# A two-way cross-attention kernel: setup opens with Wk's transposes and batch 0's keys, and batch 0's values are made by block products

## The chip, the cores and the metric

The kernel runs on one NeuronCore of one Trainium2 chip, in float32. The metric is the device time of one execution in microseconds. Five engines work in parallel from instruction streams of their own and meet through semaphores: PE (TensorE, matmuls, with PEld for its weight loads), DVE (VectorE), ACT (ScalarE), POOL (GpSimd) and SP (SyncE, which here only issues DMA transfers; ACT and POOL issue some too).

## The reference

There are 16 batches. `x` is 16 x 100 x 640; the context is 16 x 722 x 384, of which 718 rows are encoder rows and the last four are token rows. There are 8 heads of 80.

```python
enc, ca = ctx[:, :718, :], ctx[:, 718:, :]
query, keyt, valt = x @ Wq, enc @ Wk, enc @ Wv
hs = mha(query, keyt, valt)                       # 100 queries, 718 keys
ca_q1 = einsum('btc,th->bch', ca, Wq_ca)[:, indices, :]
ca_hs1 = mha(ca_q1, x, x)                         # second branch, first attention
ca_hs2 = mha(ca_hs1 @ Wq, ca @ Wk_ca, ca @ Wv_ca) # second attention, four keys
out = (hs + ca_hs2) @ Wout + b_out + x
```

The second branch is folded with weights: products of Wk_ca, Wq and the tokens (`k2`, `m`) are made once for all batches.

## The kernel before, in words

Each batch's encoder rows, transposed, are held as three thirds of 240 rows by three blocks of 128 channels (`a_raw(enc, u, c)`). Keys are computed as kT (channels on partitions, in five chunks of 128: four of packed heads and a last one for what is left of the heads), values as vs (rows on partitions, in two halves of 120 of each third).

**Two ways to the same products.** The direct way runs one matmul for each of the nine pairs of a third and a channel block, as in `first_keys` (L627, matmuls recorded at L609) and `first_values` (L414, L421). The other way is by blocks: `Values` (L456) and `Keys` (L499) walk a plan of 15 products in place of 18. Operands of these are sums of blocks: of the encoder input, by `enc_sums` (L527, recorded at L548, on POOL, thirteen for a batch), and of the weights, by `weight_sums` (L552, recorded at L572, on DVE, twelve each for Wv and Wk). A product is two matmuls; what it gives is copied by ACT or added by DVE into kT or vs. `go(n)` issues the next n products of the plan.

**Setup.** It runs from the top of the function to the batch loop at L1386:

- Loads. SP issues most, in the order of the text (`in_order`), ACT issues the six of Wv. Eight completion semaphores are used in turn by all loads from SP and ACT.
- Five matmuls on zeros (L1258), then `first_values` for four of batch 0's six blocks of rows (24 matmuls), and beside them Wv's block sums on DVE. Three of Wv's sums have no room of their own yet and go to `wv_there` (L397), which batch 1's value products read; ACT copies them home in batch 1 (L1531).
- `k2` (30 matmuls), masked by DVE (L1279); five `m_ps` tiles of five matmuls (L1293), each copied by DVE (L1301) and stored by SP; `keys(m)` (L765), in which POOL masks the five m tiles (L770).
- `Second` is the second branch of a batch: `products` makes y_ps (five matmuls, L798) and DVE reduces it to g; `scores1` (L826) is seven operations of POOL on 100 x 800 (L833, L840); `softmax1` is a maximum on DVE by two transposes and reductions (L722 to L752) and a subtraction (L850); `exponentials1` is on ACT (L853); `softmax2` makes z_ps on PE (L860) and divides it on DVE (L871).
- Fifteen transposes turn Wk back from its packed transposed form (w_ps, L1316); DVE copies Wq into its packed order (L1327, L1335, fifteen copies); then `first_keys` (45 matmuls, the last nine of them `last_keys`), va_ps (L1360) and the 25 matmuls of `queries` (L585).

Up to L1385 a scheduler of the framework decides the order on each engine; from there on (`manual_schedule`) the order of the text is the order on every engine.

**The batch loop.** For each batch: three groups of `scores` (L659), between them DVE's running maxima (`larger`, L1416 and L1428), then `softmax2`, the next batch's `products`, and a stretch in which value products of this batch and key products of the next alternate on PE while the first softmax runs on DVE and ACT (`Maximum`, `subtract`, `exponential`), then `last_keys`, r_ps (row sums, L1586) and a_ps (L1604). Batch 0 has a branch of its own: it makes the remaining 12 value matmuls directly (L421 again), and only batch 1's keys by blocks.

**Accumulators.** PSUM tiles come from three rings of two: `pair` (two banks each), `psumk` and `psum1` (one bank each); `psum` takes from them in turn in setup. A tile of a ring is free when the last reader of the tile two before it has finished: `z_ps`, `y_ps` and the two halves of v_psD all come from `psum1`.

## Time and profile before

| | |
|---|---|
| time, median of three runs | 928.01 us (927.03 to 928.19) |
| profiled execution | 927.66 us, span 925.9 us |
| PE busy | 917.3 us of the span (99%) |
| DVE, ACT, POOL busy | 650.4, 375.4, 620.9 us |
| 0 to 28.42 us (to the end of m_ps) | PE busy 26.32 us, DMA 257 GB/s |
| 28.42 to 60.86 (to batch 0's scores) | PE busy 32.01 us, DMA 140 GB/s |
| 60.86 to 100.71 (batch 0) | PE busy 39.15 us, DVE 30.64, POOL 33.64 |
| 100.71 to 156.80 (batch 1) | PE busy 56.09 us of 56.09 |

The chain of waits lists, backwards from the last instruction, what each step waited for; its rows are start, length, engine, tile and line. The timeline lists the instructions of each engine with start, busy time, line, operation, tiles, shape and number, and behind them in brackets the idle time ahead and what ended it. Times are from the start of the span. PE's matmuls leave two records each.

### The profile page before, as it was taken

What the parts mean: (1) busy time and instruction counts of PE and PEld (TensorE: products, weight loads), DVE (VectorE), ACT (ScalarE), POOL (GpSimd) and SP (SyncE); (2) the same over time, 40 slices, a digit from 0 to 9 for tenths busy, and PEclk for the clock granted to TensorE, in tenths of its full rate; (3) what the DMA queues carried; (4) which work ended last, traced back from release to release, by engine and by line L of the source; (5) the groups of instructions that cost most, each with busy time, mean ns of one, the idle gap of its engine ahead of it and who ended that gap; (6) DMA issues with size and microseconds to landing.
All of it is one profiled execution on the core that took longest, in us unless ns stands there. A gap on an engine that the chain in (4) does not pass through costs nothing.

```text
span 925.9 us, 26078 instructions
## 1 busy us (share of the span) xinstructions
PE 917.3 (99%) x11163; PEld 778.3 (84%) x11163; DVE 650.4 (70%) x1116; ACT 375.4 (41%) x649; POOL 620.9 (67%) x646
## 2 busy tenths in 40 slices
PE   9999999999999999999999999999999999999998
PEld 6997879788887979888798887988888888888865
DVE  2358896878729786685966759578792887828783
ACT  2244534434424453532434334344541445425451
POOL 5748788566945878477684856745796566955624
PEclk9999999999999999999999999999999999999999
DMA  8613352051401504140131402204140151401331
GB/s 265 201 47 87 73 120 73 6 142 34 109 12 37 138 6 110 43 123 20 49 94 43 132 12 74 72 12 133 43 109 10 34 139 36 109 12 44 86 84 32
DMA packets 68956, 69.50 MB, mean 75 GB/s; under 512 B 26088, under 2 KB 62632, under 8 KB 68840
## 3 DMA queue, kind: packets, MB, share of 16 engines
q1 hardware_dynamic: 67512, 66.51, 26.9%
q8 instruction: 88, 1.44, 0.6%
q10 hardware_dynamic: 864, 0.98, 0.3%
q0 software_dynamic: 464, 0.34, 0.2%
q14 instruction: 28, 0.23, 0.1%
HBM read 62.14 MB, written 8.94 MB: 77 GB/s over the span
## 4 chain that ended last, share of the span: by engine, by line
PE 96%; DVE 2%; DMA 1%; ACT 0%; issue 0%; POOL 0%; ACTq 0%; DVEq 0%
PE s_ps L659 12%; PE v_psA L480 10%; PE v_psB L480 8%; PE kT_ps L609 8%; PE k_psA L511 8%; PE a_ps L1604 7%; PE q_ps L585 7%; PE k_psB L511 6%; PE r_ps L1586 4%; PE v_psC L480 3%; PE k_psC L511 3%; PE v_ps L421 2%; PE y_ps L798 2%; PE o_psy L1127 2%; PE v_psD L480 2%; PE v_psE L480 2%
## 5 line engine op out<-in xcount | busy, mean ns | idle before, releaser
L833 POOL TENSOR_TENSOR e<-ca,g 100x800 f32<-100x800 f32 x64 | 99.2, 1560 | 95.6 <-DVE most L1416 90.7
L548 POOL TENSOR_TENSOR enc<-enc 128x240 f32<-128x240 f32 x135 | 104.3, 782 | 19.4 <-ACT qp L593 10.1
L480 PE MATMUL v_psA<-wv_sb,enc 128*120 128x320 f32 x352 | 109.6, 434 | 0.1
L840 POOL TENSOR_TENSOR e<-e,e 100x800 f32<-100x800 f32 x48 | 97.7, 2035 | 3.8
L659 PE MATMUL s_ps<-qp,kT 32*120 32x100 f32 x3072 | 97.5, 263 | 0.0
L659 PEld LDWEIGHTS s_ps<-qp,kT 32*120 32x120 f32 x3072 | 94.7, 179 | 2.1 <-issue 0.2
L480 PE MATMUL v_psB<-wv_sb,enc 128*120 128x320 f32 x296 | 91.7, 432 | 0.0
L1404 DVE TENSOR_TENSOR st<-st,over 120x1600 f32<-120x1600 f32 x47 | 89.9, 1913 | 0.0
L511 PE MATMUL k_psA<-enc,wk_sb 128*128 128x240 f32 x360 | 87.8, 367 | 0.6 <-DVE kT L451 0.5
L511 PEld LDWEIGHTS k_psA<-enc,wk_sb 128*128 128x128 f32 x360 | 68.2, 190 | 17.7 <-DVE kT L451 0.9
L480 PEld LDWEIGHTS v_psA<-wv_sb,enc 128*120 128x120 f32 x352 | 63.3, 183 | 23.0 <-DVE vs L451 1.0
L1416 DVE TENSOR_TENSOR most<-most,st 120x800 f32<-120x800 f32 x64 | 64.8, 1013 | 23.3 <-ACT st L681 22.2
L1412 ACT ACTIVATE st<-st 120x1600 f32<-120x1600 f32 x48 | 74.0, 1541 | 8.4 <-DVE st L1404 8.0
L1428 DVE TENSOR_TENSOR most<-st 120x800 f32<-120x800 f32 x16 | 16.9, 1059 | 81.1 <-ACT st L687 81.1
L511 PE MATMUL k_psB<-enc,wk_sb 128*128 128x240 f32 x300 | 73.1, 366 | 0.1
L480 PEld LDWEIGHTS v_psB<-wv_sb,enc 128*120 128x120 f32 x296 | 54.2, 183 | 21.7
L1604 PE MATMUL a_ps<-st,vs 120*64 120x100 f32 (+1 forms) x1536 | 69.5, 250 | 0.0
L585 PE MATMUL q_ps<-xT,wq_sb 128*128 128x200 f32 x400 | 69.1, 333 | 0.0
L1604 PEld LDWEIGHTS a_ps<-st,vs 120*64 120x64 f32 (+1 forms) x1536 | 66.4, 137 | 2.7 <-issue 2.7
L585 PEld LDWEIGHTS q_ps<-xT,wq_sb 128*128 128x128 f32 x400 | 67.9, 190 | 0.2
L940 POOL TENSOR_TENSOR hs<-hs,pb 128x500 f32<-128x500 f32 x48 | 65.5, 1364 | 3.8
L687 ACT COPY st<-s_ps 120x800 f32<-120x800 f32 x64 | 49.7, 829 | 44.0 <-PE s_ps L659 44.0
(195 smaller groups left out, 1861.3 us busy)
## 6 DMA issues: line engine op xcount, KB each, us to landing
pb<-p_d SPq DMA_DIRECT2D x32, 400.0 KB
enc<-in_enct SPq DMA_DIRECT2D x30, 240.0 KB
enc<-in_enct SPq DMA_DIRECT2D x15, 360.0 KB
xT<-in_xt SPq DMA_DIRECT2D x8, 500.0 KB
rest<-in_enct SPq DMA_DIRECT2D x31, 120.0 KB
xn<-in_x SPq DMA_DIRECT2D x11, 320.0 KB
wide_d<-p_d SPq DMA_DIRECT2D x16, 200.0 KB
pb<-wide_d SPq DMA_DIRECT2D x16, 200.0 KB
```

Of the source, the lines that this page charges most:

```text
L480: nc.tensor.matmul(at[0][j][:KN, : H // 2], a_form(self.enc, f)[:, j * KN : (j + 1) * KN], wv_there.get(f, wv_sb[:, W_AT[f]]), start=first ...
L511: nc.tensor.matmul(at[:, i * KT : (i + 1) * KT], wk_sb[:, W_AT[f], i], a_form(self.enc, f), start=(first and i == 0), stop=last, skip_grou ...
L548: first = nc.gpsimd.tensor_tensor(out, left, right, op)
L585: nc.tensor.matmul(q_ps[:, : 2 * S].rearrange("p (j s) -> p j s", j=2), wq_sb[:, c, n * P : (n + 1) * P], xT[:, :, c, :], start=(c == 0), ...
L609: nc.tensor.matmul(bank[:, i * KT : (i + 1) * KT], weights[c], a_raw(enc, u, c), start=(i == 0 and c == 0), stop=(c == CC - 1), skip_group ...
L659: nc.tensor.matmul(s_ps[bank][:n, 256 * a + lo : 256 * a + lo + rhs.shape[-1]], kT[rows, c, u, j * KN : (j + 1) * KN], rhs, start=bank not ...
L833: first = nc.gpsimd.tensor_tensor(to, self.ca[:, t, :].unsqueeze(1).to_broadcast([S, NH, S]), g[:, :, t].unsqueeze(2).to_broadcast([S, NH, ...
L840: nc.gpsimd.tensor_tensor(e, e, to, ALU.add)
L940: nc.gpsimd.tensor_tensor(self.hs2, self.hs2, to, ALU.add)
L1404: return engine.tensor_tensor(st[i], st[i], top.over[:KN].unsqueeze(1).to_broadcast([KN, 2, ROWS]), ALU.subtract,)
L1412: nc.scalar.activation(st[i], st[i], AF.Exp, scale=SCALE)
L1604: nc.tensor.matmul(wides[64 * e : 64 * e + 64, h // 2], slot(i, h, FIRST[e], 64), st[i // 2][: KEYS[i], i % 2, h * S : (h + 1) * S], start ...
```

## The change

- The hand-written order holds from the beginning of the function; `in_order` and the `issue_after` groups go.
- Loads: Wk (transposed, packed by head) comes first, its four even heads on ACT's queue, and on SP's, behind the three thirds of channel block 0 of batch 0's encoder input, the four odd heads and the rest; then the other thirds, the tokens, Wk_ca, Wq transposed, Wv in one transfer, x, Wq and ca_0. Wv_ca goes into the room of Wq transposed once m_ps is made. Batch 1's encoder input is loaded ahead of m_ps.
- PE begins (behind the five matmuls on zeros) with `turn_back` of chunks 0 and 1 and with `first_keys`, which now loops over the channel blocks outside and the chunks inside, 36 matmuls, with chunks 2 to 4 turned back in the middle. The transposes' identity lies in `e1`, which is why the fills of `e1` and `most` come later.
- DVE then makes Wk's sums (both parts), POOL the thirteen encoder sums of batch 0. k2 and m_ps follow. Wv's twelve sums go between the m copies, three behind each of the last four. Then `last_keys(0)`, Wq's fifteen copies, `products`, `copy`, `scores1`, the masks and encoder sums of batch 1, `queries`, va_ps and `softmax1`.
- `first_values`, `wv_there` and the branch of batch 0 are removed. Batch 0 takes the general path: behind its scores come two value and two key products, then `softmax2`, the next `products`, and the rest as in other batches.

The diff, cut to its core:

```diff
+def packed(to, w, h):
 
     rows = w.rearrange("(h k) n -> h k n", h=NH)
-    for h in range(NH):
-        at, c = 32 * (h // 2), 2 * (h % 2)
-        load(
-            out=to[at : at + 32, c : c + 2],
-            in_=rows[h, :64].rearrange("(v k) n -> k v n", v=2),
-        )
-    load(out=to[:, 4], in_=w.rearrange("(h k) n -> h k n", h=NH)[:, 64:])
-
-
-
-
-
-
-
-
-
-
-
-
-
-
+    at, c = 32 * (h // 2), 2 * (h % 2)
+    return {
+        "out": to[at : at + 32, c : c + 2],
+        "in_": rows[h, :64].rearrange("(v k) n -> k v n", v=2),
+    }
...
+    ctx.enter_context(tc.manual_schedule(engines=engines))
...
-    wvca_sb = enc_tile("wvca").rearrange("p f k -> p (f k)")[:, : CC * H].rearrange(
+    wvca_sb = wout_sb.rearrange("p c n -> p (c n)")[:, : CC * H].rearrange(
         "p (c n) -> p c n", c=CC
     )
+    wkt_sb = kT.rearrange("p c u k -> p c (u k)")[:, :, :CAD]
...
-    def load_first(lo, hi, u, cols):
-
-        for c in range(lo, hi):
-            k = u * (KT - 1)
-            in_order(
-                nc.sync.dma_start(
-                    out=a_raw(enc, u, c)[:, cols],
-                    in_=enct[0][:, c, k + cols.start : k + cols.stop],
-                )
-            )
-
-    load_first(0, CC, 1, slice(0, KN))
-    for g in range(2):
-        for c in range(CC):
-            nc.scalar.dma_start(
-                out=wv_sb[:, 2 * c + g],
-                in_=wv[c * P : (c + 1) * P, g * (H // 2) : (g + 1) * (H // 2)],
-            )
-    load_first(0, CC, 1, slice(KN, KT))
-    load_first(0, CC, 2, slice(0, KT))
+    for h in range(0, NH, 2):
+        nc.scalar.dma_start(**packed(wkt_sb, wkt, h))
+    for c in range(CC):
+        if c == 1:
+            for h in range(1, NH, 2):
+                nc.sync.dma_start(**packed(wkt_sb, wkt, h))
+            nc.sync.dma_start(
+                out=wkt_sb[:, 4], in_=wkt.rearrange("(h k) n -> h k n", h=NH)[:, 64:]
+            )
+        for u in range(3):
+            nc.sync.dma_start(
+                out=a_raw(enc, u, c),
+                in_=enct[0][:, c, u * (KT - 1) : u * (KT - 1) + KT],
...
-    in_order(nc.sync.dma_start(out=wqt_sb, in_=wqt.rearrange("(c p) r -> p c r", p=P)))
-    load_first(0, CC, 0, slice(0, KT))
+    nc.sync.dma_start(out=wqt_sb, in_=wqt.rearrange("(c p) r -> p c r", p=P))
+    nc.sync.dma_start(
+        out=wv_sb[:, : 2 * CC].rearrange("p (c g) n -> p c (g n)", g=2),
+        in_=wv.rearrange("(c p) n -> p c n", p=P),
+    )
     xT = inp.tile([P, 2, HC, S], F32, tag="xT", name="xT_0", bufs=1)
-    in_order(nc.sync.dma_start(out=xT, in_=xt[0:2].rearrange("b p c s -> p b c s")))
-    ca_0 = small.tile([S, T, S], F32, tag="ca", name="ca_0")
-    in_order(nc.sync.dma_start(out=ca_0, in_=cas[0].unsqueeze(0).to_broadcast([S, T, S])))
-    load_packed(
-        lambda **ends: in_order(nc.sync.dma_start(**ends)), wkt_sb[:, :, :CAD], wkt
-    )
+    nc.sync.dma_start(out=xT, in_=xt[0:2].rearrange("b p c s -> p b c s"))
     halves = [t[:, u] for t in [scores_tile(f"wq_{i}") for i in range(NP)] for u in range(2)]
     room = halves.pop()
     wq_in = [t[:, :H] for t in halves]
     for c in range(HC):
-        in_order(nc.sync.dma_start(out=wq_in[c], in_=wq[c * P : (c + 1) * P]))
-    in_order(nc.sync.dma_start(out=wvca_sb, in_=wvca.rearrange("(c p) n -> p c n", p=P)))
-
-
-
+        nc.sync.dma_start(out=wq_in[c], in_=wq[c * P : (c + 1) * P])
+    ca_0 = small.tile([S, T, S], F32, tag="ca", name="ca_0")
+    nc.sync.dma_start(out=ca_0, in_=cas[0].unsqueeze(0).to_broadcast([S, T, S]))
...
+    ident = e1[:, :P]
...
-    room_v = xn_tile("wv_there")
-    wv_there = {5: bias[:, : H // 2], 14: bias[:, H // 2 :], 7: room_v[:, : H // 2]}
...
-                    wv_there.get(f, wv_sb[:, W_AT[f]]),
+                    wv_sb[:, W_AT[f]],
...
+    def turn_back(c, copy):
+        w_ps = psum(f"w_ps_{c}")
+        for cc in range(CC):
+            nc.tensor.transpose(
+                w_ps[:, cc * P : (cc + 1) * P], wkt_sb[:, c, cc * P : (cc + 1) * P], ident
+            )
+        copy(
+            wk_sb[:, c % 2 : 6 : 2, c // 2] if c < HC - 1 else wk4,
+            w_ps[:, : CC * P].rearrange("p (a n) -> p a n", a=CC),
+        )
+
     def first_keys(enc):
-        for n in range(HC - 1):
-            banks = [psum(f"kT_ps_0_{n}_{k}") for k in range(2)]
-            weights = [wk_sb[:, 2 * c + n % 2, n // 2] for c in range(CC)]
-            copies = chunk_keys(n, banks, weights, enc)
-        last_keys(0, enc)
-        return copies[-1]
+
+        banks = {}
+        copies = nc.scalar.copy, nc.vector.tensor_copy
+
+        def begin(n, get):
+            if get is pair:
+                both = pair(f"kT_ps_0_{n}")
+                banks[n] = [both[:, k] for k in range(2)]
+            else:
+                banks[n] = [get(f"kT_ps_0_{n}_{k}") for k in range(2)]
+
+        for n in range(2):
+            turn_back(n, copies[n])
+            begin(n, pair)
+        for c, chunks in ((0, (0, 1)), (0, (2, 3)), (1, range(4)), (2, range(4))):
+            if len(banks) < 4 and 2 in chunks:
+                for n in (2, 3, 4):
+                    turn_back(n, copies[n % 2])
+                begin(2, psum1)
+                begin(3, psumk)
+            for n in chunks:
+                for bank, thirds in zip(banks[n], ((0, 1), (2,))):
+                    for i, u in enumerate(thirds):
+                        nc.tensor.matmul(
+                            bank[:, i * KT : (i + 1) * KT],
+                            wk_sb[:, 2 * c + n % 2, n // 2],
+                            a_raw(enc, u, c),
+                            start=(i == 0 and c == 0),
+                            stop=(c == CC - 1),
+                            skip_group_check=True,
+                        )
+        for n in banks:
+            for bank, thirds in zip(banks[n], ((0, 1), (2,))):
+                w = len(thirds)
+                nc.scalar.copy(
+                    kT[:, n, thirds[0] : thirds[0] + w],
+                    bank[:, : w * KT].rearrange("p (u k) -> p u k", u=w),
+                )
...
-    for i in (1, 4, 2, 5):
-        first_values(i, enc, (act, act))
-    weight_sums(nc.vector, wv_sb, there=wv_there)
+    first_keys(enc)
+    nc.vector.tensor_reduce(
+        qmask, ident.rearrange("p (r u k) -> p u r k", r=RG, u=2), AX.XY, ALU.add
+    )
+    nc.gpsimd.memset(most[96:, :], LOW)
+    nc.gpsimd.memset(e1[96:, :], LOW)
+    weight_sums(nc.vector, wk_sb, False)
+    weight_sums(nc.vector, wk_sb, True)
+    enc_sums(enc)
...
+    enc_next = load_rest(1, load_enc(1))
     for c in range(HC):
...
-        copied = nc.vector.tensor_copy(
+        nc.vector.tensor_copy(
             m_sb[c].rearrange("p (b h t) -> p h b t", h=NH, t=T),
             m_ps.rearrange("p (h b t) -> p h b t", h=NH, b=B),
         )
         nc.sync.dma_start(out=m_d[c], in_=m_sb[c])
+        if c:
+            weight_sums(nc.vector, wv_sb, part=slice(3 * c - 3, 3 * c))
+    nc.sync.dma_start(out=wvca_sb, in_=wvca.rearrange("(c p) n -> p c n", p=P))
     second = Second(0, xT, ca_0)
     keys(load_m(0))
-    summed = second.products()
+    last_keys(0, enc)
+    for c in range(HC):
+        for u in range(2):
+            nc.vector.tensor_copy(
+                wq_sb[:, c, 2 * u * P : 2 * (u + 1) * P].rearrange(
+                    "p (v r k) -> p r v k", v=2, r=RG
+                ),
+                wq_in[c].rearrange("p (r u k) -> p r u k", r=RG, u=2)[
+                    :, :, u, :64
+                ].rearrange("p r (v k) -> p r v k", v=2),
+            )
+        nc.vector.tensor_copy(
+            wq_sb[:, c, 4 * P :].rearrange("p (h k) -> p h k", h=NH),
+            wq_in[c].rearrange("p (h k) -> p h k", h=NH)[:, :, 64:],
+        )
+    second.products()
     second.copy()
     second.scores1()
     keys(load_m(1))
-
-    for c in range(HC):
-        w_ps = psum(f"w_ps_{c}")
-        for cc in range(CC):
-            nc.tensor.transpose(
-                w_ps[:, cc * P : (cc + 1) * P], wkt_sb[:, c, cc * P : (cc + 1) * P], ident
-            )
-        act(
-            wk_sb[:, c % 2 : 6 : 2, c // 2] if c < HC - 1 else wk4,
-            w_ps[:, : CC * P].rearrange("p (a n) -> p a n", a=CC),
+    enc_sums(enc_next)
...
+    second.softmax1()
...
-        if b == 0:
-            enc_sums(enc)
-            now.softmax1()
         st.append(scores(b, 0, tiles))
-        waiting = b > 0 and late
-        if b == 0 or late:
+        waiting = late
+        if late:
             now.exponentials1()
         nc.vector.tensor_tensor(most[:KN], st[0][:, 0], st[0][:, 1], ALU.max)
         st.append(scores(b, 1, tiles))
         larger(1)
         st.append(scores(b, 2, tiles))
+        vv = Values(b, e_in, V_PLAN if b + 1 < B else END_PLAN)
+        if b + 1 < B:
+            kk = Keys(b + 1, enc)
+        if b == 0:
+            seen = larger(2)
+            now.exponentials1()
+            vv.go(2)
+            kk.go(2)
         now.softmax2()
         if b + 1 < B:
             second.products()
             second.copy()
         if b == B - 1:
             now.scores2()
-        seen = larger(2)
+        if b:
+            seen = larger(2)
         top = Maximum(most, f"{b}", True)
+
         if b + 1 < B:
-            kk = Keys(b + 1, enc)
-
-        if b == 0:
-            second.scores1()
-            m_next = load_m(b + 2)
-            kk.go(3)
-            top.go(3)
-            first_values(3, e_in, (act, act), get=bank)
-            top.go(1)
-            first_values(0, e_in, (act, act), (0, 1), bank)
-            second_next, enc_next = loads()
-            enc_next = load_rest(b + 2, enc_next)
-            now.scores2()
-            kk.go(2)
-            top.go()
-            kk.go(3)
-            now.softmax3()
-            kk.go(3)
-            now.spread2()
-            subtract(0)
-            exponential(0)
-            kk.go(2)
-            subtract(1)
-            kk.go(3)
-            exponential(1)
-            subtract(2)
-            exponential(2)
-            last_keys(b + 1, enc)
-            keys(m_next)
-            enc_sums(enc_next, slice(LATE_SUMS.start))
-            now.values2()
-        elif b + 1 < B:
-            vv = Values(b, e_in)
...
-            both(3)
+            both(3 if b else 1)
...
-                for f in list(wv_there):
-                    nc.scalar.copy(wv_sb[:, W_AT[f]], wv_there.pop(f))
```

More of the change, by code (lines that the diff above doesn't have):

```diff
@@ L402 @@
     m_d = dram.tile([HC, P, B * HT], F32, name="m_d")
-    most = const.tile([P, ROWS], F32, name="most")
-    nc.gpsimd.memset(most[96:, :], LOW)
-    e1 = const.tile([P, ROWS], F32, name="e1")
-    nc.gpsimd.memset(e1[96:, :], LOW)
     y_there = const.tile([S, NH, HT + 1], F32, name="y")
     nc.gpsimd.memset(y_there[:, :, HT:], 1.0)
-    def first_values(i, enc, engines, halves=(0, 1), get=psum):
-        u, j = KC[i]
-        for g in halves:
-            engine = engines[g]
-            v_ps = get(f"v_ps_0_{i}_{g}")
-            for c in range(CC):
-                nc.tensor.matmul(
-                    v_ps[:KN, : H // 2],
-                    a_raw(enc, u, c)[:, j * KN : (j + 1) * KN],
-                    wv_sb[:, 2 * c + g],
-                    start=(c == 0),
-                    stop=(c == CC - 1),
-                )
-            engine(
-                vs[:, j, 2 * u + g, :, :D],
-                v_ps[:KN, : H // 2].rearrange("p (h d) -> p h d", d=D),
-            )
     class Blocks:
@@ L550, in enc_sums, with weight_sums @@
         return begun
-    def weight_sums(engine, w, late=None, there={}):
-        at = lambda f: there.get(f, w[:, W_AT[f]])
+    def weight_sums(engine, w, late=None, part=slice(None)):
+        at = lambda f: w[:, W_AT[f]]
         raw = lambda c, g: w[:, 2 * (c - 1) + g - 1]
-        for f, left, right in (
+        sums = (
             (0, raw(1, 2), raw(1, 1)),
@@ L1486 @@
             store(seen)
-            last.load(seen)
+            if last:
+                last.load(seen)
             if b == B - 2:
@@ L1540 @@
         else:
-            vv = Values(b, e_in, END_PLAN)
             last.place()
@@ L1564 @@
             vv.go(5)
-        paired = 0 < b and last.b in PAIRED
+        paired = last and last.b in PAIRED
         late = b % 2 == 0 and not paired
```

85 lines of the change are left out of this document (28 added, 57 removed).

## The prediction

> **What bounds the kernel now.** I read the page first, then the chain of waits up to batch 1, then the timeline of each engine over that stretch.
>
> ```profile
> span 925.9 us, 26078 instructions
> ...
> PE 917.3 (99%) x11163; PEld 778.3 (84%) x11163; DVE 650.4 (70%) x1116; ACT 375.4 (41%) x649; POOL 620.9 (67%) x646
> ...
> PE 96%; DVE 2%; DMA 1%; ACT 0%; issue 0%; POOL 0%; ACTq 0%; DVEq 0%
> ```
>
> TensorE is busy for 99% of the span and carries 96% of the chain that ended last. So a change counts as far as it shortens what PE executes or changes how long PE stands still. In both programs PE executes the same products in the same order from batch 1's scores on; I take whatever offset exists there as carried one for one to the end. The question is thus when batch 1's scores begin, which is 100.71 us now. The chain up to there (start, length, what):
>
> ```profile
> 1.75 4.73 DMA wv_sb<-in_wv
> ...
> 19.15 1.90 PE k_ps L1270 x60
> 21.05 0.51 issue
> 21.56 6.86 PE m_ps L1293 x50
> ...
> 28.67 1.11 POOL m L770 x4
> ...
> 30.93 0.98 PE w_ps L1316 x7
> 31.91 18.23 PE kT_ps L609 x90
> 50.14 2.06 PE va_ps L1360 x60
> 52.20 8.65 PE q_ps L585 x50
> 60.86 7.35 PE s_ps L659 x240
> 68.20 0.68 PE z_ps L860 x56
> 68.88 1.14 PE y_ps L798 x10
> ...
> 70.86 0.81 PE k_psB L511 x4
> ...
> 72.48 6.47 PE v_ps L421 x24
> ...
> 90.36 3.65 PE kT_ps L609 x18
> 94.00 1.52 PE r_ps L1586 x64
> ...
> 100.71 7.38 PE s_ps L659 x240
> ...
> 111.01 1.08 PE v_psB L480 x4
> ```
>
> PE is the chain almost throughout; the rows also tell where it isn't. (A matmul leaves two records, so x24 are 12 matmuls and x4 one block product of two.) The setup's 24 value matmuls stand before 19.15; the 12 of batch 0 give their price, 6.47/12 = 0.539 us. Starting at 3.58 (below), 24 of them would end at 16.5, so 2.6 us were lost. Further losses are the 0.51 at the masked keys before m_ps, about 0.7 of the 1.11 at y_ps (transposes filled some of it), and 1.7 in batch 0's middle: 94.00 − 68.20 = 25.8 against 0.68 + 1.14 + 15 key products of 0.81 + 6.47 + 3.65 = 24.1. In sum before loses 2.6 + 0.5 + 0.7 + 1.7 = 5.5 us on the way to batch 1.
>
> **PE work removed and added.** Gone are 36 direct matmuls for batch 0's values, 36 × 0.539 = 19.4 us. Added are 15 block products of 1.08 each (row at 111.01), 16.2 us. The 45 matmuls of batch 0's keys, the 15 transposes, k2, m, y, va, q and scores are the same in number and only stand elsewhere. Net −3.2 us. This is the whole gain.
>
> **The start.** The first rows of the timeline:
>
> ```profile
> 0.83 3.65 ACTq L318 DMA_DIRECT2D wv_sb<-in_wv  x6
> ...
> 1.14 2.50 PE L1258 MATMUL idle_ps<-vaT 128*128 128x128 f32 x10 [1.14 <-DVE vaT L1255]
> ...
> 3.58 1.42 PE L421 MATMUL v_ps<-wv_sb,rest 128*120 128x320 f32 x2
> ...
> 4.79 1.27 PE L421 MATMUL v_ps<-wv_sb,enc 128*120 128x320 f32 x2
> ...
> 7.67 0.70 PE L421 MATMUL v_ps<-wv_sb,rest 128*120 128x320 f32 x2
> ...
> 7.88 0.49 DVE L572 TENSOR_TENSOR bias<-wv_sb 128x320 f32<-128x320 f32 x1 [0.19 <-DMA wv_sb<-in_wv]
> ```
>
> Before's first real matmul waits for one block of the keys' input and one wv load, and goes at 3.58. After, the first real work is the transposes of Wk's chunk 0, and a chunk's rows come from all four even heads, so it waits for the fourth transfer on ACT's queue. In the built program eight completion semaphores serve the loads in turn, and that fourth transfer waits, on ACT, until the first has landed; nothing else is queued behind it there but the copies, which need it anyway. Before has the same shape one transfer later: the fifth wv transfer waits for the first, and its first reader, the DVE sum into bias, starts at 7.88. Bounds for the first transpose: 5.7 (the first landing at about 3.5, since the matmul at 3.58 waited for it, then the 2.2 us which that load took from the end of its own issue) and 7.9. The row at 1.75 shows that 4.73 us can lie between an issue and its landing there. I take 7.25, nearest to the 7.88, less one issue (some 0.45) and a little for smaller transfers. Start shift: 7.25 − 3.58 = +3.7 us.
>
> The bytes do not rescue it:
>
> ```profile
> GB/s 0 0 32 296 296 100 180 347 357 190 225 201 237 79 232 372 396 400 411 394 396 393 385 352 379 393 310 235 228 203 170 86 121 76 260 322 348 355 290 386
> DMA packets 5912, 7.82 MB, mean 261 GB/s; under 512 B 1707, under 2 KB 4367, under 8 KB 5911
> ```
>
> The columns are 0.75 us each; summed, some 0.54 MB have arrived by 4.5 us and 0.94 MB by 6.0. The four even heads (0.39 MB) share that with three thirds of encoder input (0.37 MB) and odd heads of SP's queue, so by bytes alone 5.5 to 6 is the earliest. The Trainium skill ("DMA: Bandwidth & Descriptors", section "Issuing engines are not separate DMA queues") says that starting transfers on several engines saves only sequencer time, since all run on the same 16 engines. By that rule the ACT/SP split buys nothing and the four heads land with the bytes, at about 5.7, and the sum below would be 1.6 us smaller; the row of before's fifth transfer says 7.25.
>
> **The slow first matmuls.** The two pairs that stand at 3.58 and 4.79 took 1.42 and 1.27 us, the pair at 7.67 took 0.70: PE ran at half pace for 4.1 us after its first real work. That loss is inside before's 2.6. After, PE ends the five warm-up matmuls at 3.64 and idles to 7.25, then works without waits; half pace for about 3.8 us then costs 1.9. Bounds: 0 if the pace follows time since the warm-up, 3.2 if it takes the 6.5 us from 1.14 to 7.67 anew. I take 1.9, since the 4.1 us began with work, as these do. The Trainium skill ("TensorE: Matmul & The Clock Gate", "Part 1: The HAM clock gate") has the array at half rate after an idle window of about 3.4 us and until about 3.4 us of sustained work; the sum by that is an estimated 1.7. The granted clock on the page reads 9s throughout and doesn't show it; by it alone the cost would be nothing.
>
> **Setup after the start.** Transposes (0.98/7 each or a little less, 1.7 to 2.1 as now) and 36 key matmuls (four fifths of 18.23) fill PE to 26. Two stops: k2_ps can't take its accumulator until ACT has emptied the key banks (0.5), and m_ps waits for the masked keys as now (0.6; row at 21.05: 0.51). m_ps ends at 35.5, the last nine key matmuls (3.65, as in the row at 90.36) at 39.2. Then y_ps needs the five masked m tiles from POOL. Here the rows that decide are these:
>
> ```profile
> 30.33 5.41 POOL L770 TENSOR_TENSOR m<-m,hmask 128x64 f32<-128x64 f32 x1 [0.25 <-PE y_ps L798]
> ...
> 30.46 0.49 DVE L1327 COPY wq_sb<-wq 128x256 f32<-128x256 f32 x2
> ...
> 33.16 2.43 DVE L572 TENSOR_TENSOR wk_sb<-wk_sb 128x256 f32<-128x256 f32 x7
> ...
> 35.70 3.03 POOL L833 TENSOR_TENSOR e<-ca,g 100x800 f32<-100x800 f32 x2
> ...
> 45.95 1.88 POOL L840 TENSOR_TENSOR e<-e,e 100x800 f32<-100x800 f32 x1
> ...
> 47.86 1.01 DVE L722 STREAM_TRANSPOSE turned<-e 128x800 f32<-128x800 f32 x1 [12.27 <-POOL e L840]
> ...
> 52.94 2.08 DVE L572 TENSOR_TENSOR wk_sb<-wk_sb 128x256 f32<-128x256 f32 x5
> ...
> 55.97 0.99 DVE L850 TENSOR_TENSOR e<-e,over 100x800 f32<-100x800 f32 x1
> ...
> 67.58 2.17 DVE L1416 TENSOR_TENSOR most<-most,st 120x800 f32<-120x800 f32 x2 [1.04 <-ACT st L681]
> ...
> 68.24 1.55 ACT L687 COPY st<-s_ps 120x800 f32<-120x800 f32 x2 [0.69 <-PE s_ps L659]
> ...
> 70.40 3.23 DVE L1416 TENSOR_TENSOR most<-most,st 120x800 f32<-120x800 f32 x2
> ```
>
> The row at 28.67 has four of POOL's masks (L770) in 1.11; the single one at 30.33 took 5.41, exactly while DVE ran fifteen SBUF copies (the row at 30.46 begins them) and seven SBUF sums (33.16 to 35.59), and it ended with them. After, the change puts twelve wv sums of 0.4 between the m copies (three behind each of the last four), and the fifteen wq copies (0.18 apart, 30.46 to 33.16) directly behind them. Three sums and a copy take 1.8 to 2 us where PE makes a tile in 1.37 (6.86/5), so the last m copy, which could end at 36.3, ends at 38.2; three more sums and the copies hold DVE to 42.1, and POOL's last mask comes at about 42.4. PE has 0.9 of y_ps to do from 39.2 and waits 2.1. If POOL isn't held, the mask is there at 38.6 and the cost is 0; if the copies run on at the pitch of 30.46, 2.5.
>
> q (8.65), va (2.06) and scores (7.35) follow as now. wv (loaded behind wqt), wq, ca_0 and enc_1 arrive later than now, but at the 7.82 MB of the first 30 us all setup loads are in by some 33 us, each ahead of their first use at 31 (wv), 39 (wq), 43 (ca_0) and 57 (enc_1); wvca's load, queued on SP behind the m stores, is needed at 51. POOL's thirteen encoder sums lie beside the 36 key matmuls. I cost these moves at nothing; if wv were late, the m copies queued behind its sums would be late with it, one for one.
>
> **Batch 0.** After scores PE goes straight to v_psA. Its accumulator pair is freed by the first of the two ACT copies at 68.24 (0.8 each); before, z_ps and y_ps (1.82) stand between, after, nothing: wait 1.0. Then two value and two key products (3.8), z_ps, y_ps, and v_psD. That one needs the bank of z_ps, which DVE empties when it divides z; and on DVE this division is queued behind softmax1 and the maxima. DVE's side, counted from the end of y_ps of batch 0: 0.6 to the first POOL step; scores1 on POOL 47.83 − 35.70 = 12.1; softmax1 from the transpose at 47.86 to the end of L850 at 56.96, less the wk sums in between (2.08, earlier now), 7.0; five maxima of 1.1 to 1.6 (rows at 67.58 and 70.40, two each), taken nearer the second, since POOL's encoder sums now run beside them, 7.3; division 0.7: 27.7. PE's side from the same point: 8.65 + 2.06 + 7.35 + 1.0 + 3.8 + 0.68 + 1.14 = 24.7. PE waits 3.0. With maxima at 1.1 it is 0.7 to 1.0; if encoder sums delay softmax1 too, 4.5. Smaller stops at the copies of products later in the batch: 0.7, taken at under half of before's 1.7, since value products of 1.08 leave DVE more time than its key products did alone.
>
> Gone too are batch 1's three ACT copies of wv_there, which no row of the chain waits for: 0.
>
> **The sum.** After loses 1.9 + 0.5 + 0.6 + 2.1 + 1.0 + 3.0 + 0.7 = 9.8, before 5.5: +4.3. With the start +3.7 and the work −3.2: +4.8; the 0.2 to 0.3 by which my pieces of before fall short of its 100.71 come off (they recur): +4.5. The profiled run took 927.66 (span 925.9 and 1.76 around it), 0.35 under the median of 928.01; 927.66 + 4.5 = 932.2, against the median 932.5. I predict 932.5.
>
> **Rivals.** 0.2%, about what a measurement of this kernel tells from no change, is 1.9 us.
> - *Faster: POOL and DVE don't hold each other.* Then the mask costs 0 instead of 2.1 and the maxima run at 1.1 throughout, so that v_psD waits 0.7 instead of 3.0: −4.4, which leaves +0.1. With a first transpose before 5.7 (−1.6, and 0.4 less of half pace) it decides: −1.9, 926.0. For it: the 5.41 is one row, and the slow maxima at 70.40 are one pair. Against: at 67.58, with POOL's sums just over, the same maxima took 1.1, and at 70.40, beside POOL's scores1, 1.6. Chance 0.12.
> - *No change to measure.* The transfers share out evenly and the start comes by bytes, at 5.7: 1.6 less, and with 0.4 less of half pace and one of the two waits on POOL and DVE halved +1.3. 929.3. Chance 0.15.
> - *Later still.* The fourth head lands at 8 or later behind SP's transfers, half pace lasts the full 6.5 us, the z wait is 4.5: +7 to +8. 935.5. Chance 0.15.
> - My forecast, its own range 930 to 934.5: 0.58.
>
> So faster 0.12, same 0.15, slower 0.73; the range 927.0 to 936.5 leaves a tenth below and a little above.
>
> **What will show it.** In the changed profile: the first transpose at 7.25 behind a load of kT, and key matmuls at double length until about 11; m_ps starting near 28.7; POOL's last L764 mask near 42 and a PE wait of 2 before y_ps; a wait of 1 behind batch 0's scores and of 3 at v_psD with z's division on DVE as the releaser; batch 1's scores near 105.2. The prediction is wrong if the transposes start before 6, if POOL's masks take 0.3 beside the wq copies, or if the batches behind batch 0 shift by themselves.

## The result

The changed kernel takes 933.64 us (median of four runs, 933.25 to 934.06), the kernel before 928.1 beside it: a ratio of 1.006, interval 1.0043 to 1.0078. So it is 5.5 us slower, where 4.5 were forecast (932.5, range 927.0 to 936.5). The profiled execution took 933.25 us, span 931.5, against 925.9 before.

The chain of waits of the changed kernel up to batch 1's scores (start, length, what; the rows left out between 42.80 and 69.44 are the rest of POOL's first scores, softmax1 and the maxima, each behind the other):

```profile
0.82 2.82 DMA kT<-in_wkt
...
3.66 3.69 DMA kT<-in_wkt
...
7.45 1.51 PE w_ps L581 x6
...
28.92 2.96 PE m_ps L1290 x20
...
42.80 3.05 POOL e L827 x2
...
54.99 1.02 DVE turned L716
...
67.91 1.37 DVE most L1389
...
69.44 0.44 DVE z L865
...
70.01 2.46 PE v_psD L431 x4
72.47 1.19 PE k_psD L462 x4
73.66 1.08 PE v_psA L431 x4
...
96.30 3.64 PE kT_ps L560 x18
...
106.43 7.28 PE s_ps L653 x240
```

Batch 1's scores begin at 106.43, where they began at 100.71: +5.7, which is the whole difference of the spans (5.6): from there to the end both take 825.1 to 825.2 us. In before's chain PE stood at nearly every step from 6.5 us on. Here the chain leaves PE twice: at the start it runs over two transfers one behind the other, and from 31.9 to 70.0 over DVE and POOL, until v_psD of batch 0 has its bank. (From 39.11 to 42.78 the chain has only a row of issue; the timeline below names what POOL waited for there, the sum g.)

The changed kernel's timeline at the start (start, busy time, line and tile, and in brackets the idle time ahead and what ended it): the two records of a key matmul took 1.00 us at 9.85 and 0.57 from 11.96 on, so PE ran at about half pace at first. (A transpose leaves one record, not two: w_ps has 15 in all.)

```profile
9.85 1.00 PE L613 MATMUL kT_ps<-rest,wk_sb 128*128 128x240 f32 x2
...
11.96 0.57 PE L613 MATMUL kT_ps<-rest,wk_sb 128*128 128x240 f32 x2
```

The same timeline behind m_ps, down to v_psD:

```profile
38.48 1.38 DVE L523 TENSOR_TENSOR wv_sb<-wv_sb 128x320 f32<-128x320 f32 x3
38.64 0.47 POOL L764 TENSOR_TENSOR m<-m,hmask 128x64 f32<-128x64 f32 x1 [1.43 <-DVE m L1298]
...
39.31 1.12 PE L792 MATMUL y_ps<-m,xT 128*100 128x96 f32 x10
...
39.78 0.48 DVE L1311 COPY wq_sb<-wq 128x256 f32<-128x256 f32 x2
...
42.48 0.24 DVE L801 TENSOR_REDUCE g<-y_ps 100x32 f32<-100x96 f32 x1
...
42.80 3.04 POOL L827 TENSOR_TENSOR e<-ca,g 100x800 f32<-100x800 f32 x2 [3.69 <-DVE g L801]
...
59.90 1.34 PE L431 MATMUL v_psA<-wv_sb,enc 128*120 128x320 f32 x4 [0.91 <-ACT st L681]
...
70.01 2.46 PE L431 MATMUL v_psD<-wv_sb,enc 128*120 128x320 f32 x4 [4.26 <-DVE z L865]
```

POOL's last mask came at 38.64, so y_ps and q followed the keys without a pause. g, the sum of y_ps, came only at 42.48, behind Wq's copies on DVE, 2.1 us after y_ps was done, and POOL's first scores waited for g. And v_psD waited 4.26 us for z's division.

The stretch from 65 to 80 us in both kernels (length; busy time and count for PE, PEld, DVE, ACT and POOL; then granted clock, DMA share, GB/s), before and after:

```profile
65.00:80.00 15.00, 15.00 (x225) 12.42 (x219) 12.25 (x20) 9.59 (x19) 11.94 (x8) 1.00 0.14 37
```

```profile
65.00:80.00 15.00, 10.74 (x43) 8.07 (x42) 14.24 (x26) 4.44 (x9) 14.20 (x10) 0.89 0.04 6
```

PE is busy for 10.74 of 15 us, where it was busy throughout, and its granted clock falls to 0.89: behind the 4.26 us of idleness v_psD ran at half pace (2.46 for 1.08) and k_psD partly so (1.19 for 0.81). A product that starts behind a wait takes 1.33 at full pace, as runs below show, so about 1.5 of these 1.8 us are the pace.

The account, in the prediction's terms, which leaves some 0.3 of the 5.7 open: start +3.9 (7.45 against 3.58); PE work −3.2; stops behind the start 2.1 (half pace) + 0.6 (k2) + 0.5 (masked keys) + 0 (y_ps) + 0.9 (v_psA) + 4.3 (v_psD) + 1.8 (half pace behind it) = 10.2 against before's 5.5.

### The profile page after: what moved, and what is told of

Read it like the earlier page. It is cut to its first block, busy times and chain, and to the rows that moved or that the text cites. A ratio compares the mean times of both kernels' runs of the same rounds, so it can differ in the third digit from the quotient of the medians.

```text
span 931.5 us, 26067 instructions
## 1 busy us (share of the span) xinstructions
PE 915.0 (98%) x11151; PEld 777.8 (83%) x11151; DVE 662.6 (71%) x1129; ACT 372.3 (40%) x640; POOL 631.3 (68%) x659
## 4 chain that ended last, share of the span: by engine, by line
PE 93%; DVE 3%; POOL 1%; issue 1%; DMA 1%; ACT 1%; DVEq 0%; POOLq 0%; ACTq 0%
PE s_ps L653 11%; PE v_psA L431 11%; PE v_psB L431 9%; PE k_psA L462 8%; PE a_ps L1550 7%; PE k_psB L462 6%; PE q_ps L536 6%; PE kT_ps L560 6%; PE r_ps L1532 4%; PE v_psC L431 4%; PE k_psC L462 3%; PE v_psD L431 2%; PE o_psy L1121 2%; PE v_psE L431 2%; PE y_ps L792 2%; PE kT_ps L613 2%
## 5 line engine op out<-in xcount | busy, mean ns | idle before, releaser
L431 PE MATMUL v_psA<-wv_sb,enc 128*120 128x320 f32 x384 | 119.6, 434 | 1.0 <-ACT st L681 0.9
L499 POOL TENSOR_TENSOR enc<-enc 128x240 f32<-128x240 f32 x144 | 111.6, 785 | 8.0
L431 PE MATMUL v_psB<-wv_sb,enc 128*120 128x320 f32 x320 | 99.2, 432 | 0.0
L431 PEld LDWEIGHTS v_psA<-wv_sb,enc 128*120 128x120 f32 x384 | 69.0, 183 | 26.1 <-ACT st L681 1.2
L431 PEld LDWEIGHTS v_psB<-wv_sb,enc 128*120 128x120 f32 x320 | 58.6, 183 | 23.4
L404 ACT COPY vs<-v_psA 120x640 f32<-120x640 f32 x48 | 33.3, 693 | 84.7 <-PE v_psA L431 84.7
```

The lines of the kernel that those rows point to most:

```text
L431: nc.tensor.matmul(at[0][j][:KN, : H // 2], a_form(self.enc, f)[:, j * KN : (j + 1) * KN], wv_sb[:, W_AT[f]], start=first, stop=last, skip ...
L499: first = nc.gpsimd.tensor_tensor(out, left, right, op)
```

## The experiments

The theory after this reading had three parts: the start is late because one transfer waits for another's landing; PE's pace is low because PE had idled; and batch 0 waits at a chain of POOL and DVE work that begins with y_ps. The rivals were that the bytes set the start, that the slow pace belongs to something else, and that gains ahead of the chain, or in it, are given back. Nine kernels were run, each an edit of the changed one. Each was compared with the kernel before on the same chip, whose median was 928.1 for the first four of them, 927.6 for the two with the key chunks' order and 927.4 for the last three; distances to before are taken from these, and the changed kernel's is +5.5. Each distance is uncertain by 0.8 to 1.6 us, so a gain of under some 2 us is not clear of noise by the time alone; there the traces' rows carry the argument.

**Wk's even heads first on both queues.**

```diff
-    for h in range(0, NH, 2):
+    for h in (0, 4):
         nc.scalar.dma_start(**packed(wkt_sb, wkt, h))
+        nc.sync.dma_start(**packed(wkt_sb, wkt, h + 2))
```

> The changed kernel, but the four even heads of Wk go first on both queues, two on ACT's and two on SP's, ahead of the three thirds of encoder input; no one of them then waits for an earlier landing. My theory: the first transposes stood at 7.45 because the fourth transfer on ACT's queue was issued only after the first had landed at 3.64 (two landings one behind the other), not because of bytes, since only 0.13 to 0.03 MB arrived in each of the last microseconds ahead of 7.4. Then the first transpose comes at 3.8 to 4.5, everything behind it moves along, and the time falls by 3.0 to 3.6 us against the changed kernel's 933.6, to about 930.3. Rival one, bytes and landing of small transfers are what takes 7 us: the start stays at 6 or later, less than 1.2 us gained. Rival two, what is won at the start is given back at v_psD of batch 0, since the chain through POOL and DVE hangs on loads: start at 4, time within 1 us of 933.6.

Measured: 930.69 us, +2.6 to before, so 2.9 won; ratio to before 1.003 (1.0018 to 1.0041). The chain of waits:

```profile
1.28 3.19 DMA kT<-in_wkt
...
4.71 1.51 PE w_ps L582 x6
...
67.14 2.46 PE v_psD L432 x4
...
103.47 7.28 PE s_ps L654 x240
```

The first transpose stands at 4.71 instead of 7.45, behind one transfer instead of two, and batch 1's scores begin 2.96 earlier. ACT's four issues took 3.16 us in the changed kernel, and the two that are left to it take 0.90. So the start was set by the wait of a transfer for a landing. This run by itself doesn't part that from the bytes, since the four heads now also go ahead of the encoder input; the changed kernel's DMA rate does (GB/s by microsecond from 0 on):

```profile
GB/s 0 17 254 285 265 209 129 32 194 277 277 275 175 379 369 397 415 397 402 405 402 389 403 405 378 397 387 271 306 335 302 84 270 221 62 236 33 217 55 205
```

From 6 to 7 and from 7 to 8 us, around the end of PE's wait at 7.45, the queues moved 129 and 32 GB/s, less than in the microseconds on either side, so it was not bytes that PE waited for. What was won at the start was carried through. The wait at v_psD (67.14, 4.27 us) moved along and stayed as long.

**Twelve more matmuls on zeros ahead of the first transposes.**

```diff
-    for _ in range(5):
+    for _ in range(17):
         nc.tensor.matmul(idle_ps[:, :P], idle, idle, start=True, stop=True)
```

> The changed kernel with 17 instead of 5 matmuls on zeros ahead of the first transposes, so that PE has work from 1.14 to about 7.3 us and doesn't idle for 3.8. My theory: the first key matmuls ran at half pace (1.17, 1.00 and 0.74 us a pair of records against 0.57 later) until about 11.5 only because PE had idled; then with the longer warm-up they take 0.57 from the start, m_ps begins about 1.9 us earlier than 28.92, and the time falls by 1.5 to 2.0, to about 931.8. Rival, the slow pace belongs to the first 4 us of real data, or to loads that land late: no change in m_ps's begin and in the time (933.6, within 0.5).

Measured: 932.14 us, +4.0, 1.5 won; ratio 1.0051 (1.0035 to 1.0066). The timeline's start:

```profile
1.14 5.83 PE L1250 MATMUL idle_ps<-vaT 128*128 128x128 f32 x34 [1.14 <-DVE vaT L1247]
...
7.49 0.84 PE L581 MATMUL w_ps<-e,kT 128*128 128x128 f32 x6 [0.52 <-issue]
...
9.09 0.57 PE L613 MATMUL kT_ps<-rest,wk_sb 128*128 128x240 f32 x2
```

The transposes take 0.84 instead of 1.51, the key matmuls 0.57 from the first on, and m_ps begins at 27.26 instead of 28.92. The low pace at the start is a matter of PE's idleness. In this profile half of the gain was lost again behind v_psD, where the half pace lasted longer (k_psD 1.60 and v_psA 1.51 us on the chain, for 1.19 and 1.08 in the changed kernel), so that batch 1's scores begin only 0.8 earlier. The span as a whole was 1.5 shorter all the same (930.0 for 931.5); the other 0.7 came behind batch 1's begin, where the runs differ by up to 1.2, and has no account.

**The last two maxima behind z's division.**

```diff
         if b == 0:
-            seen = larger(2)
             now.exponentials1()
...
-        if b:
-            seen = larger(2)
+        seen = larger(2)
```

> The changed kernel with batch 0's last two maxima on DVE behind the division of z_ps and the sum into g, as in all other batches, instead of ahead of them. My theory: v_psD of batch 0 waits 4.26 us for the bank that the division frees, and the division stands behind five maxima of 1.0 to 1.4. Without the two the division ends 2.7 us earlier, PE waits 1.6 and does not fall to half pace behind it (v_psD took 2.46 for 1.08, k_psD 1.19 for 0.81): in sum 4.2 to 4.6 us, about 929.2. Rival one, the pace behind the wait has another cause: only 2.7, about 930.9. Rival two, the maxima pushed back delay the first softmax and what is won comes back as a wait at r_ps or at the products' additions: less than 1.5 us gained.

Measured: 933.12 us, +5.0, 0.5 won; ratio 1.0054 (1.0038 to 1.007). The timeline:

```profile
68.28 1.33 PE L431 MATMUL v_psD<-wv_sb,enc 128*120 128x320 f32 x4 [1.43 <-DVE z L865]
...
76.94 1.34 PE L431 MATMUL v_psA<-wv_sb,enc 128*120 128x320 f32 x4 [1.45 <-DVE vs L402]
...
80.49 1.08 PE L462 MATMUL k_psE<-enc,wk_sb 128*128 128x240 f32 x4 [0.92 <-DVE vs L402]
```

The second rival was right. v_psD waits 1.43 instead of 4.26 and runs at full pace, but the value product at 76.94 and the key product at 80.49 now wait for additions on DVE (1.45 and 0.92 us), and k_psE begins at 80.49, where it began at 80.39 in the changed kernel (the whole of this execution lay 1.1 us later up to m_ps, so some 1.0 of the gain was left there). My reading: DVE has the same work to do before the products can go on, in whatever order. What counts is when that work begins.

**Wv's sums ahead of k2.**

```diff
     weight_sums(nc.vector, wk_sb, False)
+    weight_sums(nc.vector, wv_sb)
     weight_sums(nc.vector, wk_sb, True)
...
-        if c:
-            weight_sums(nc.vector, wv_sb, part=slice(3 * c - 3, 3 * c))
```

(and Wv's load ahead of Wq transposed's)

> The changed kernel with Wv's twelve block sums on DVE behind the first part of Wk's sums, ahead of k2, instead of three behind each m copy, and Wv loaded ahead of Wq transposed so that they find it. My theory: the twelve sums push the last m copy and Wq's fifteen copies back by about 2, g of batch 0 waits behind those copies (y_ps was done at 40.4, g began at 42.48), and with g the whole chain through POOL's first scores, softmax1, the maxima and the division of z_ps. Without them g comes at about 40.5, v_psD waits about 2.2 instead of 4.26 and doesn't fall to half pace: 3.5 to 4.0 us, about 929.9. Rival, POOL's encoder sums, which then run beside the twelve sums, get so late that masks, scores1 and the chain are no earlier, or k2's masks wait for DVE: less than 1.5 us gained.

Measured: 933.5 us, +5.4, nothing won; ratio 1.0058 (1.0043 to 1.0074). The timeline of DVE and PE:

```profile
19.21 8.92 DVE L523 TENSOR_TENSOR wv_sb<-wv_sb 128x320 f32<-128x320 f32 x12 [1.09 <-DMA wv_sb<-in_wv]
...
30.38 6.91 PE L1291 MATMUL m_ps<-wq,wout_sb 128*128 128x128 f32 x50 [2.04 <-DVE wq L1279]
...
41.94 0.26 DVE L801 TENSOR_REDUCE g<-y_ps 100x32 f32<-100x96 f32 x1 [1.10 <-PE y_ps L792]
```

The rival was right, in its second form. Wv landed at 19.2, the twelve sums took 8.92 us beside POOL's encoder sums (0.74 each instead of 0.48), and m_ps waited 2.0 for the masked keys. What the m copies won, k2 lost; g came 0.5 earlier, v_psD still waited 3.0 (4.26 in the changed kernel), and it ran at half pace behind that wait too (2.46).

**Wq's copies on ACT.** The piece of the chain that the last run did not reach, by itself; the loop of fifteen copies also moves ahead of `last_keys(0, enc)`:

```diff
-            nc.vector.tensor_copy(
+            nc.scalar.copy(
                 wq_sb[:, c, 2 * u * P : 2 * (u + 1) * P].rearrange(
```

> The changed kernel with nothing else altered than that Wq's fifteen copies run on ACT, ahead of the last keys. It measures what these copies ahead of g cost by themselves. My theory: g begins at 40.5 instead of 42.48 and the whole chain to the division comes 2.0 earlier; v_psD waits 2.2 instead of 4.26 and the half pace behind it goes: 2.0 from the chain and up to 1.8 from the pace, 929.8 to 931.6. Rival, as in the run with Wv's sums moved, the gain is given back: within 0.7 of 933.6.

Measured: 931.37 us, +3.9, 1.6 won (batch 1's scores begin 1.9 earlier, at 104.49); ratio 1.0042 (1.0029 to 1.0055). The timeline:

```profile
40.16 0.26 DVE L801 TENSOR_REDUCE g<-y_ps 100x32 f32<-100x96 f32 x1 [0.61 <-PE y_ps L792]
...
67.68 1.33 PE L431 MATMUL v_psD<-wv_sb,enc 128*120 128x320 f32 x4 [2.92 <-DVE z L865]
...
68.97 1.97 PE L462 MATMUL k_psD<-enc,wk_sb 128*128 128x240 f32 x4
...
70.73 2.06 PE L431 MATMUL v_psA<-wv_sb,enc 128*120 128x320 f32 x4
```

g follows y_ps at once, and v_psD waits 2.92. Here the gain stays, since the chain's whole rest begins earlier. The pace behind the wait did not recover as expected: v_psD's 1.33 is full pace, as at 68.28 in the run with the maxima, but the key and value products behind it took 1.97 and 2.06, where 0.97 and 1.24 are usual on the timeline. In the chain that is 1.9 us more than at full pace, about as much as in the changed kernel, so the gain is the chain's alone.

**Batch 0's keys as cover behind m_ps again.** Chunks 0 and 1 ahead of k2, chunk 2 between m_ps and y_ps, chunk 3 and the last keys behind y_ps:

```diff
     keys(load_m(0))
-    last_keys(0, enc)
+    more_keys(2, enc)
...
     second.products()
     second.copy()
     second.scores1()
+    more_keys(3, enc)
+    last_keys(0, enc)
+    weight_sums(nc.vector, wk_sb, True)
```

(the loop of `first_keys`, not shown, changes with it, and the last five of Wk's sums on DVE move too, from ahead of k2 to behind g)

> The changed kernel with the order of its key chunks alone changed: chunks 0 and 1 (18 matmuls) ahead of k2 and m_ps, then chunk 2, y_ps, chunk 3 and the last keys; the late part of Wk's sums stands behind g. The same matmuls in all. My theory after the first four runs: batch 0's wait at v_psD, and the waits on DVE that took its place when the division came earlier, come from one chain, g, POOL's first scores, softmax1, maxima, division, products' additions, which begins with y_ps; the changed kernel puts all of batch 0's key matmuls (14.6 us in first_keys) ahead of y_ps where the kernel before had them behind it as cover. Here y_ps ends near 33 instead of 40.3, POOL's first scores begin near 35 instead of 42.8, v_psD waits less than 0.5, PE keeps its pace, and the time falls by 5 to 6.5 us, to about 928. Rival one, m_ps now waits for Wq transposed, whose load lands at 20 or later, and the gain is lost there: 1 to 3 us gained. Rival two, batch 0's middle is bound by DVE's sum of work however early the chain begins (as the additions in the run with the maxima behind suggest): v_psD waits less, later products wait on DVE, less than 2 us gained.

Measured: 928.26 us, +0.7, 4.8 won; ratio 1.0005 (0.9996 to 1.0014). The chain of waits, and two of PE's waits:

```profile
7.98 1.51 PE w_ps L581 x6
...
33.20 0.96 PE y_ps L797 x10
...
66.79 0.80 PE v_psD L431 x2
...
102.14 7.28 PE s_ps L658 x240
```

```profile
PE k_psE L462 <- DVE vs L402: 0.7, 1, 0.7
...
PE v_psD L431 <- ACT y L818: 0.2, 1, 0.2
```

Now the same matmuls, in another order, cost as much as the kernel before, though the start is even later (7.98). y_ps stands at 33.20 (33.03 on the timeline) instead of 39.31, v_psD waits 0.2 for another reason, and DVE's additions stop PE for 0.7 once. This is the run that settles the matter: the chain from y_ps through POOL's first scores to the division needs PE work behind y_ps to hide it, and the change had moved all 45 key matmuls, 18.2 us of such work, ahead of it (the 14.6 of the expectation leave out the last nine). Here 18 of them, 7.3 us, stand behind y_ps again. Neither of the two other things that moved explains it: g (at 36.70) still stood behind Wq's copies, 2.6 after y_ps was done, and Wk's last sums had ended at 27.85 in the changed kernel, 0.7 before DVE's next work, so they had not held up g.

**Both orders together, then two more matmuls on zeros, then Wq's copies on ACT.** Three chunks ahead of k2 and one behind m_ps, with the heads on both queues:

> The order of the run before, but with three chunks (27 matmuls) ahead of k2, and Wk's even heads first on both queues as in the run that had them so. If start and chain are separate losses, their gains add: first transpose at 3.9, y_ps ends near 32.5, batch 1's scores begin near 96.5, and the time is 923 to 925.5, under the kernel before's 928.1 by about 4. If both meet at the loads (Wq transposed, Wv, Wq come no earlier), the gain at the start is given back in m_ps or y_ps: 927 to 929.

Measured: 926.68 us, −0.9; ratio 0.9992 (0.9983 to 1.0001), which neither of the two forecasts met. Next, `range(7)` for the matmuls on zeros:

> The run that had both orders (three chunks ahead of k2, even heads first on both queues; 926.7), with seven instead of five matmuls on zeros, so that PE works from 1.14 to the first transposes at 4.6 without the pause of 1.0. My theory: PE's pace rises about 3.4 us after unbroken work begins (seventeen such matmuls took 5.83 us, which fits half a microsecond each up to about 4.5 and a quarter behind), so the first key matmuls run at full pace, k2 begins near 18 instead of 20.2, and the time falls by 1.5 to 2.2, to about 924.8. Rival, m_ps then waits for the load of Wq transposed or batch 0's chain through DVE gives it back: less than 0.7.

Measured: 926.3 us, −1.1; ratio 0.999 (0.9982 to 0.9999). And with Wq's copies on ACT, ahead of chunk 3:

> The same, and Wq's fifteen copies run on ACT, ahead of chunk 3's keys, instead of on DVE ahead of g. My theory: g begins right behind y_ps (2 us earlier, as the copies no longer stand ahead of it), POOL's first scores, softmax1 and the division come 2 earlier, the wait of 1.8 at v_psD and most of the waits on DVE's additions behind it go: 1.5 to 3 us less than the run with seven warm-up matmuls, about 922.5. Rival, the copies on ACT take longer than on DVE, wait for Wq's load, and hold up the key copies, y or q: nothing gained or a loss.

Measured: 924.21 us (923.74 to 925.1), −3.2; ratio 0.9966 (0.9953 to 0.9978). The chain of the first of the three, its timeline and one of PE's waits, a wait in the second's timeline, and a chain row and the waits of the third:

```profile
4.62 1.51 PE w_ps L582 x6
...
100.01 7.28 PE s_ps L659 x240
```

```profile
36.15 0.24 DVE L807 TENSOR_REDUCE g<-y_ps 100x32 f32<-100x96 f32 x1
36.31 7.47 DVE L524 TENSOR_TENSOR wk_sb<-wk_sb 128x256 f32<-128x256 f32 x5
...
36.47 3.33 POOL L833 TENSOR_TENSOR e<-ca,g 100x800 f32<-100x800 f32 x2 [3.70 <-DVE g L807]
```

```profile
PE v_psD L432 <- DVE z L871: 1.8, 1, 1.8
```

```profile
10.40 0.52 PE L582 MATMUL w_ps<-e,kT 128*128 128x128 f32 x3 [1.37 <-DMA kT<-in_wkt]
```

```profile
97.64 7.28 PE s_ps L659 x240
```

```profile
PE v_psA L432 <- ACT st L687: 1.0, 1, 1.0
...
PE v_psD L432 <- DVE z L871: 0.4, 1, 0.4
```

The two gains did not add in full: the first lies 1.6 below the chain's run alone, where 2.9 had been won by the heads alone. With three chunks ahead of k2 and the fourth ahead of y_ps, only the last nine key matmuls (3.65 us) stand behind y_ps, half of the cover of the run before; y_ps comes no earlier (32.98), g comes at 36.15, still behind Wq's copies, and v_psD waits 1.8 again. The two matmuls on zeros moved the first transposes to full pace, but then PE waited 1.37 at 10.40 for the rest of Wk, the rows of the last chunk, which were issued at 5.18 and landed at 10.26; 0.2 to 0.4 was left, which is not clear of noise. With the copies off DVE the wait at v_psD is 0.4, and the kernel is 3.2 us faster than the one before. That is the fastest of these runs; its remaining waits, 1.0 at v_psA and 1.1 for loads at the start, were not tried.

## Why the prediction was right, and where its steps failed

- *PE bounds the kernel, and an offset at batch 1 is carried to the end.* Right. Over all runs the median time less the begin of batch 1's scores in the profile lies between 826.1 and 827.5 us (928.1 − 100.71 = 827.4; 933.64 − 106.43 = 827.2; 924.21 − 97.64 = 826.6).
- *Work −3.2.* Value products took 1.08 each in batch 0 and key products 0.81, as forecast; no run measured this term alone.
- *Start at 7.25.* 7.45, for the reason given: a transfer issued behind a landing at 3.64, its own landing 3.7 later. The rival by bytes, 5.7, fell. Two queues did help (4.71): the chain then has one landing ahead of the transposes instead of two. That the wait was for a completion semaphore comes from the built program; no run varied it. The Trainium skill ("DMA: Bandwidth & Descriptors", "Issuing engines are not separate DMA queues") has several issuing engines save only issue time; here spreading four transfers over two queues, ahead of the others, saved 2.7 us, which is the wait for a landing, in a stretch where the queues moved 129 GB/s and less.
- *Half pace 1.9.* 2.1, and 1.7 of it could be removed with work for PE in the pause.
- *k2 0.5 and masked keys 0.6.* 0.6 and 0.5.
- *y_ps waits 2.1 for POOL's mask.* Wrong: 0. I had POOL held from the first of the last sums to the end of Wq's copies, by the row of 5.41 us in before. POOL's masks got in between the sums (0.47 to 0.53 each), and the last was done 0.7 before the copies began.
- *v_psD waits 3.0.* 4.26. This is the other side of the same error. The chain's end I had right within half a microsecond: y_ps end at 42.6, then 27.7, is 70.3; measured is 69.86. That was luck in part: y_ps itself was done at 40.4, and g, not the mask, waited 2.1 behind Wq's copies, a wait that my 27.7 didn't have. So PE came to v_psD 1.6 earlier than I had it (65.75 against 67.3) and waited there instead. The two stops together were forecast at 5.1 and measured at 4.3.
- *Half pace behind the wait.* Not foreseen, 1.8. I had priced the low pace at the start and hadn't asked whether another idle stretch of 3 us or more would bring it back. This is the term that was missing. It is larger than the whole distance between 932.5 and 933.64, and the sum came so near only because two of its terms were too large: the two stops by 0.8 and the smaller stops by 0.7. That is luck.
- *v_psA 1.0.* 0.9. *Smaller stops 0.7.* None: from 73.66 to 96.30 each row of the chain is PE. *With maxima at 1.1, a wait of 0.7 to 1.0.* By my own rows, 27.7 less 1.8 against 24.7, it is 1.2, so the rival that used 0.7 was priced half a microsecond too fast.
- *Of the rivals,* "POOL and DVE don't hold each other" was right on what the mask cost, though for another reason (no mask ran beside Wq's copies, so the case of the 5.41 did not come up), and wrong on the maxima, which took 1.3 to 1.4 us on the chain beside POOL's encoder sums; it needed a start before 5.7, and that did not come. What none of my cases named is why the chain was late at all: not the lock, but the order of PE's work.

## What to carry to other kernels

When work is moved to another place on the bounding engine, ask what it hid where it stood: here 18.2 us of matmuls behind y_ps had covered a chain of POOL and DVE, and the same matmuls ahead of it left PE waiting, though PE had less to do. A wait that is shortened without its chain beginning earlier comes back one step on; start the chain earlier, by taking other work out of its engine's queue or by putting cover behind its first step. And price an idle stretch of PE of some 3 us or more twice, once as idleness and once as the slow pace behind it (waits of 1.4 and 1.8 us brought none here).

## What the runs showed of the hardware that was not expected

- PE's low pace has two faces in the profile. At the start the matmuls took twice their time while the granted clock read 1.00 (from 7.45 to 12 us); behind v_psD's wait the same doubling came with a granted clock of 0.89 from 65 to 80 us. The sizes of idleness were 4.26 and 3.0 us (half pace at once), 2.92 (full pace for the first product, then half for 3.8 us), 1.8 and 1.43 (none). The Trainium skill ("TensorE: Matmul & The Clock Gate", "Part 1: The HAM clock gate") has the array fall to half rate after an idle window of about 3.4 us, with a window that runs freely; the run with 2.92 us shows that less than that can do, and that the fall can come when PE is at work again.
- With continuous work from 1.14 us on, seventeen matmuls on zeros took 5.83 us. Of their 34 records 15 had started by 4.5 us and 23 by 5.5, so the pace rose near 4.5 us, after seven or eight of the matmuls.
- POOL and DVE slowed each other, now the one and now the other. In the kernel before, one mask of POOL took 5.41 us beside DVE's copies and sums. In the run with both orders it was DVE that waited: five sums of some 0.41 us took 7.47 beside POOL's first scores, which were only little slower (3.33 for two, 3.04 in the changed kernel). That they hold each other is read from the times alone, and which of the two is held when was not settled by these runs.
